# Layer 1's attention over all nodes: both row deviations multiplied into the value, gamma and beta applied to the sums

## The chip, the cores and the metric

The kernel runs on one core of a Trainium2 chip. The metric is the time of one execution in device microseconds. Before the change the median of 6 runs is 3528.72 us (3521.03 to 3540.67).

The engines are named as the profile names them: PE (TensorE matmul) and PEld (its weight load), DVE (VectorE), ACT (ScalarE), POOL (GpSimd) and SP (SyncE, which here only issues transfers). PSUM is the memory that matmuls write to.

## The reference, cut to what matters

A graph network of two layers works on 3125 nodes with 256 features and 100000 edges. Layer 1 adds to every node a sum over its neighbours (graph attention), an attention over all nodes that is linear in the queries, and then a mixture of experts. The change is in the second of these:

```python
q = _split_heads(seq @ wq.T, B, S)          # 4 heads of 64
k = _split_heads(seq @ wk.T, B, S)
v = _split_heads(seq @ wv.T, B, S)
k = _layer_norm(k, ln_k_g, ln_k_b)          # over the 64 of a head: (k - mu) * rsqrt(var + eps) * g + b
v = _layer_norm(v, ln_v_g, ln_v_b)
kv = jnp.einsum('bhsd,bhse->bhde', k, v) / S
ga = jnp.einsum('bhsd,bhde->bhse', q, kv)
return ga @ wo.T + bo
```

For each head `kv` is a 64 by 64 matrix, a sum over all nodes of the outer product of a normalized key and a normalized value.

## The kernel before, in words

**Tiles and blocks.** The 3125 nodes lie in 25 tiles of 128 rows (the last has 53). The edges are sorted by target and lie in 31 blocks (`NK`): block 0 and block 30 hold 7 gathers, every other block 28. The stage of interest is class `Layer1`; its order of instructions is written by hand, and each engine works through its own list in that order.

**A block** (`block`, L1562 to L1670) does the graph attention of its edges. At its top `run` (L1893) calls `gather` for the *next* block: 28 indirect transfers on POOL (L1555), each of 128 rows of 264 numbers, into the buffers `r0` (three of them) and `r1` (two). So gathers of the next block can start when the matmuls that read the old contents of those buffers are done (L1662, the `sums` of the block before). The block itself adds the two halves of the scores (L1581), finds maxima along runs of edges (L1590 to L1626, with PE transposes in L1594 and L1609), takes exponentials into `factors`, which lies in the PSUM tile `fixed` (L1631), multiplies the gathered rows by them (L1650: 128x4096, then 128x3072), builds one-hot matrices (L1653: `dl` compared with `self.row`, the numbers 0 to 31) and sums the messages with matmuls (L1662). `close`, `place` and `placed` add the result of the block before to the nodes (L1683, L1702, L1710).

**Units.** The other two parts of layer 1 are cut into units, generators that `yield` a nominal cost in us. `take(us)` (L1382) adds to a credit and lets units run until the credit is used up. A block calls it five times, with 2, 3, 3.5, 5 and 5 times `more` (L1616): `more` is 1.0 in block 0, 1.3 in blocks 1 to 6, and 1.0 from block 7 on (1.5 in the last ones). The queue of units begins with `keys` (the sums of `kv` over all tiles), then `mix` (folds `wo` and `wq` into them), then `mixing` (one matmul pair for each tile, which adds the attention to the nodes, L1872 and L1876), and then the experts, a group of tiles at a time, once these are complete. `run` calls `take(12)` before block 0.

**One tile of `keys`** (L1781 to L1809), as a pipeline of three steps:

- `products(t)`: the tile's transposed rows `xm` (loaded by SP, L1856, four buffers) times `wk` and `wv`, L1786, into a PSUM tile `yp` of 2x256 numbers (two buffers, shared with `place` and `mixing`). The means over a head are already taken out of the weights (L1776 to L1778).
- `normal_heads`: ACT squares (L1792), DVE sums the squares of each head (L1795), ACT takes the root (L1796), DVE the reciprocal (L1797), and then DVE multiplies by the reciprocal (L1800), by gamma (L1801) and adds beta (L1802), each over 128x512, into `h1` (two buffers). Gamma and beta of key and value lie on all partitions in an `xt` tile.
- `add(t)`: two matmuls for each tile, key against value, into `cps`, the right half of `fixed` (L1808).

PE's list has `products(t)`, then `add(t-2)`; DVE's has `normal_heads(t-1)` behind that. At the end (L1822) `cps` is scaled by 1/N and masked to the blocks of a head, and `mix` goes on from there.

`fixed` is one PSUM tile of 128x512 numbers: `self.row` in columns 0 to 31, `factors` in 32 to 255, `cps` in 256 to 511. A float32 matmul shows in the trace as two pairs of a weight load and a matmul.

Of the kernel before, what the change touches and what calls it, by code (L numbers as in the profile page):

```python
# [17 lines left out]
N, D, E = 3125, 256, 100000  # L18
P = 128
NB = 25  # L20
# [15 lines left out]
R, HD, DH = 8, 8, 32  # L36
# [7 lines left out]
def row_bc(v, n, start=0):  # L44

    return bass.AP(tensor=v.tensor, offset=v.offset + start, ap=[[0, P], [1, n]])
# [863 lines left out]
QD, QC, NQ = 32, 7, 118  # L910
# [3 lines left out]
NK = len(BQ)  # L914
# [25 lines left out]
GB = 3  # L940
# [330 lines left out]
class Layer1:  # L1271
# [290 lines left out]
    def block(self, b, part, A, N):  # L1562

        nc, C, wk, ps, B = self.nc, self.C, self.wk, self.ps, self.B
# [82 lines left out]
        for j, (s0, k, r, got) in enumerate(part):  # L1647
            n = nq * k
# [110 lines left out]
    def keys(self):  # L1759


        nc, wk, ps, C = self.nc, self.wk, self.ps, self.C
        ws = []
        xt = wk.tile([P, 2, GB * P], F32, name="xt")
        gb = xt[:, :, :P].rearrange("p j (i d) -> p j i d", i=2)
        heads = lambda x: x.rearrange("p i (h d) -> p i h d", d=64)
        for i, c in enumerate("kv"):
            w = load_k(nc, wk, self.a[f"L1_mix_w{c}T"], f"ew{i + 1}")
            for j, p in enumerate("gb"):
                nc.sync.dma_start(gb[:, j, i, :], row_bc(self.a[f"L1_mix_ln_{c}_{p}"], 64))  # L1770
            ws.append(w)
        for t in range(4):
            self.mixed_rows(t)
        for w in ws:
            mean = wk.tile([P, HD], F32, name="den").rearrange("p (i h) -> p i h", i=2)
            nc.vector.tensor_reduce(mean, heads(w), AX.X, OP.add)  # L1776
            nc.vector.tensor_scalar(mean, mean, -1.0 / 64, None, op0=OP.mult)
            nc.vector.tensor_tensor(heads(w), heads(w), mean[:, :, :, None].to_broadcast([P, 2, 4, 64]), OP.add)  # L1778
        yield 1.0

        def products(t):  # L1781
            x = self.xm.pop(t)
            kp = ps.tile([P, 2, D], F32, name="yp", bufs=2)
            for i in range(2):
                for k in range(2):
                    nc.tensor.matmul(kp[:, i, :], x[:, k, :], ws[i][:, k, :], start=(k == 0), stop=(k == 1))  # L1786
            self.mixed_rows(t + 4)
            return kp

        def normal_heads(kp):  # L1790
            sq = wk.tile([P, 2, GB * P], F32, name="h2")[:, :, :D]
            nc.scalar.activation(sq, kp, AF.Square)  # L1792
            var = wk.tile([P, HD], F32, name="den")
            v = var.rearrange("p (i h) -> p i h", i=2)
            nc.vector.tensor_reduce(v, heads(sq), AX.X, OP.add)  # L1795
            nc.scalar.activation(var, var, AF.Sqrt, bias=C.eps, scale=1.0 / 64)  # L1796
            nc.vector.reciprocal(var, var)  # L1797
            kv = wk.tile([P, 2, GB * P], F32, name="h1")[:, :, :D]
            sh = [P, 2, 4, 64]
            nc.vector.tensor_tensor(heads(kv), heads(kp), v[:, :, :, None].to_broadcast(sh), OP.mult)  # L1800
            nc.vector.tensor_tensor(heads(kv), heads(kv), gb[:, 0, :, None, :].to_broadcast(sh), OP.mult)  # L1801
            nc.vector.tensor_tensor(heads(kv), heads(kv), gb[:, 1, :, None, :].to_broadcast(sh), OP.add)  # L1802
            return kv

        def add(t, kv):
            n = P if t < NB - 1 else LAST
            for g in range(2):
                nc.tensor.matmul(self.cps[g], kv[:n, 0, g * P:(g + 1) * P], kv[:n, 1, g * P:(g + 1) * P],  # L1808
                                 start=(t == 0 and g == 0), stop=(t == NB - 1 and g == 1))  # L1809

        kp, kv = products(0), None
        yield 2.4
        for t in range(1, NB + 2):
            nxt = products(t) if t < NB else None
            if kv is not None:
                add(t - 2, kv)
# [951 lines left out]
```

## Time and profile before

| what | us |
|---|---|
| median of the 6 runs | 3528.72 |
| lowest, highest | 3521.03, 3540.67 |
| the profiled execution's own time | 3535.06 |
| its span, first to last instruction | 3533.3 |

The mean TensorE clock granted in the span is 0.825. Busy shares of the span: PE 67% (PEld 45%), DVE 50%, ACT 22%, POOL 29%. The chain of work that ended last, followed back from the end, is spread over many lines: PE 20%, "another core or an unknown queue" 13%, DVE 10%, issue 8%, ACT 3%, POOL 2%, DMA 2%.

Layer 1's blocks take the time from 1690 us to the end. In it `keys` runs from 1701 us to 1972 us, `mix` and `mixing` to about 2062 us.

How to read the views used below. In a *table of stretches* each row is a stretch of time with the busy us of each engine (and the number of instructions), the granted clock (1.00 is full), the share of the 16 DMA engines and the GB/s. In the *timeline* each row is start, duration, engine, line, operation, tiles, and in square brackets the idle time of that engine before it with what ended it: another instruction, "remote" (a semaphore that the profile cannot put down to anyone near it in time), or "issue" (nothing that the profile shows). A *view of one line* gives the number of its instructions, their duration in ns (minimum, median, maximum), first and last start, and the forms.

### The profile page before, as it was taken

The page shows a single profiled execution, that of the slowest core. Times are in us where ns is not written, and L with a number is a line of the kernel's source. Part 1 is how long each engine was busy: PE and PEld are TensorE (multiplying, and loading weights), DVE is VectorE, ACT ScalarE, POOL GpSimd, SP SyncE. Part 2 cuts the span into 40 slices and gives each one's busy share as a digit, 9 for nine tenths or more (in the row PEclk, how much of TensorE's full clock was granted, in tenths as well). Part 3 has the DMA queues.
Part 4 walks back from the last instruction along what each step waited for, and adds up shares of the span by engine and source line. Part 5 has one row for each costly group of instructions (what it writes and reads, how often), then busy time and mean ns, then how long its engine had stood idle before and what let it go on. Part 6 is the DMA issues. An engine that isn't in the chain of part 4 may idle for free.

```text
span 3533.3 us, 36506 instructions
## 1 busy us (share of the span) xinstructions
PE 2372.5 (67%) x12426; PEld 1579.8 (45%) x12426; DVE 1775.7 (50%) x4133; ACT 786.8 (22%) x1788; POOL 1026.4 (29%) x1075
## 2 busy tenths in 40 slices
PE   2788899999678999889245535535445554554576
PEld 1465544556466888544133324323223332333455
DVE  6999887566400212343266544456345446453552
ACT  2444022222211222222021112112112111121233
POOL 1000000011266000310533445365454455454400
PEclk9899999999788999899676767667668776687788
DMA  3333466332444667444522444344344344343434
GB/s 111 69 74 76 147 204 206 94 104 85 128 129 141 201 189 226 138 157 167 142 73 67 111 110 130 102 128 119 99 114 119 103 118 122 98 131 109 124 94 128
DMA packets 434699, 440.55 MB, mean 125 GB/s; under 512 B 167203, under 2 KB 380600, under 8 KB 434374
## 3 DMA queue, kind: packets, MB, share of 16 engines
q1 hardware_dynamic: 340160, 271.40, 25.7%
q0 software_dynamic: 50128, 130.98, 13.7%
q10 hardware_dynamic: 44214, 35.72, 3.8%
q8 instruction: 102, 1.67, 0.2%
q14 instruction: 95, 0.78, 0.1%
HBM read 337.49 MB, written 100.46 MB: 124 GB/s over the span
## 4 chain that ended last, share of the span: by engine, by line
PE 20%; another core or an unknown queue 13%; DVE 10%; issue 8%; ACT 3%; POOL 2%; DMA 2%; ACTq 0%; SPq 0%; DVEq 0%; POOLq 0%
PE hp L1420 7%; PE hp L2686 4%; PE yp L1480 3%; POOL r L1555 2%; PE sums L1662 2%; DVE r L1650 1%; DMA ew<-in_L_ffn_expert_w 1%; DVE own L1372 1%; ACT h L1423 1%; PE yp L1503 1%; PE hp L1412 1%; DVE ot L1351 0%; PE yp L1702 0%; DMA r<-tab,b_at 0%
## 5 line engine op out<-in xcount | busy, mean ns | idle before, releaser
L1555 POOL DMA_INDIRECT r<-tab,b_at x826 | 792.8, 960 | 1060.9 <-issue 397.4
L1420 PE MATMUL hp<-xt,ew 128*128 128x256 f32 (+2 forms) x576 | 195.7, 475 | 146.0 <-ACT h L1423 112.7
L2237 POOL DMA_INDIRECT route_x<-x,slot x50 | 50.6, 1012 | 812.8 <-DVE slot L2233 648.4
L1480 PE MATMUL yp<-ew,h 128*128 128x256 f32 x600 | 171.5, 434 | 156.3 <-issue 99.3
L2380 PE MATMUL fhp<-fxe,fw 128*128 128x256 f32 x960 | 240.3, 408 | 39.4 <-ACT fhid L2381 25.8
L1650 DVE TENSOR_TENSOR r<-r,fixed 128x4096 f32<-128x4096 f32 (+3 forms) x62 | 229.3, 3698 | 64.6 <-ACT fixed L1631 55.9
L1423 ACT ACTIVATE h<-hp,bc 128x256 f32<-128x256 f32 (+2 forms) x288 | 136.8, 481 | 556.9 <-PE hp L1420 243.6
L2380 PEld LDWEIGHTS fhp<-fxe,fw 128*128 128x128 f32 x960 | 188.1, 204 | 88.9 <-ACT fhid L2381 34.2
L2535 PE MATMUL agg<-at,py 128*128 128x512 bf16 (+4 forms) x1200 | 218.9, 336 | 1.6 <-issue 1.4
L2535 PE MATMUL agg<-at,px 128*128 128x512 bf16 (+2 forms) x1050 | 217.0, 358 | 1.9 <-DMA row_beta<-in_L_gnn_beta 1.9
L2388 PE MATMUL fyp<-fw,fhid 128*128 128x256 f32 x960 | 212.2, 379 | 0.0
L1480 PEld LDWEIGHTS yp<-ew,h 128*128 128x128 f32 x600 | 127.9, 221 | 186.9 <-issue 110.8
L1486 DVE SCALAR_TENSOR_TENSOR xs<-yp,wgt,xs 128x256 f32<-128x256 f32 x150 | 66.2, 478 | 282.8 <-PE yp L1480 171.8
L1420 PEld LDWEIGHTS hp<-xt,ew 128*128 128x128 f32 x576 | 115.6, 226 | 197.3 <-ACT h L1423 122.6
L2686 PE MATMUL hp<-wt,xt 128*128 128x512 f32 x400 | 186.6, 620 | 21.3 <-ACT xt L351 9.7
L1420 PE MATMUL hp<-h,ew 128*128 128x256 f32 (+2 forms) x576 | 178.6, 442 | 27.8 <-ACT h L1423 14.1
L2388 PEld LDWEIGHTS fyp<-fw,fhid 128*128 128x128 f32 x960 | 180.5, 190 | 22.9
L2381 ACT ACTIVATE fhid<-fhp,fb 128x256 f32<-128x256 f32 x240 | 112.6, 473 | 334.2 <-PE fhp L2380 206.8
L1662 PE MATMUL sums<-r,oh 128*32 128x264 f32 x1652 | 132.5, 439 | 39.9 <-DVE oh L1653 25.6
L2535 PEld LDWEIGHTS <-py 128*128 128x128 bf16 (+1 forms) x1200 | 111.6, 99 | 90.4 <-issue 7.2
L1420 PEld LDWEIGHTS hp<-h,ew 128*128 128x128 f32 x576 | 115.0, 220 | 74.1 <-issue 24.6
L2666 POOL DMA_INDIRECT y<-route_y,slot x50 | 49.3, 986 | 337.7 <-SPq L2637 307.2
(468 smaller groups left out, 3909.1 us busy)
## 6 DMA issues: line engine op xcount, KB each, us to landing
fw<-in_L_ffn_W SPq DMA_DIRECT2D x60, 1024.0 KB
ew<-in_L_ffn_expert_w SPq DMA_DIRECT2D x216, 256.0 KB
at<-adj SPq DMA_DIRECT2D x44, 640.0 KB
route_x<-zero SPq DMA_DIRECT2D x104, 256.0 KB
tab<-stage SPq DMA_DIRECT2D x25, 1056.0 KB
oe<-b_order ACTq DMA_DIRECT2D x117, 168.0 KB
adj<-adj_o SPq DMA_DIRECT2D x78, 250.0 KB
r<-tab,b_at POOLq DMA_INDIRECT x826
```

The lines of the kernel that those rows point to most:

```text
L1420: nc.tensor.matmul(hp[:, :W], ws[i, e][:, n, j * P:(j + 1) * P], x[:, n, :W], start=(n == 0), stop=(n == 1))
L1423: nc.scalar.activation(o[:, j, :W], hp[:, :W], AF.Relu, bias=b[:, e, j:j + 1])
L1480: nc.tensor.matmul(y[:, i - i0, :], h2[e][:, n, i * P:(i + 1) * P], ws[3, e][:, n, :], start=(n == 0), stop=(n == 1))
L1486: nc.vector.scalar_tensor_tensor(xs[:, t, :], y[:, i - i0, :], wgt[:, i, e:e + 1], xs[:, t, :], op0=OP.mult, op1=OP.add)
L1555: st = self.nc.gpsimd.indirect_dma_start(out=r[:, q, c, :], out_offset=None, in_=self.table, in_offset=bass.IndirectOffsetOnAxis(ap=self.B ...
L1650: nc.vector.tensor_tensor(rv, rv, factors[j][:, :, :, None].to_broadcast([P, n, HD, DH]), OP.mult)
L1662: mm = nc.tensor.matmul(self.sums[q * QD:(q + 1) * QD, :], oh[:, q, c, :], r[:, q, c, :], start=(s0 + c == 0), stop=(s0 + c == QC - 1))
L2380: nc.tensor.matmul(hp, w1[:, k, i * P:(i + 1) * P], xe[:, k, :], start=(k == 0), stop=(k == 1))
L2381: nc.scalar.activation(hid[:, i, :], hp, AF.Gelu, bias=b1[:, 0, i:i + 1])
L2388: nc.tensor.matmul(yp, hid[:, i, t * P:(t + 1) * P], w2[:, i, :], start=(i == 0), stop=(i == K1 - 1))
L2535: nc.tensor.matmul(agg[g][:, :cw], parts[j][:n, k, g * P:(g + 1) * P], at[:n, i, :cw], start=(k == 0 and j == 0), stop=(k == NB - 1 and j ...
L2686: nc.tensor.matmul(hp.rearrange("p r d -> p (r d)"), xt[:, k, :], wt[:, k, j * 512:(j + 1) * 512], start=(k == 0), stop=(k == 1))
```

## The change

1. `normal_heads` no longer normalizes the key. ACT copies the raw products of key and value to `h1`; DVE multiplies the two reciprocals of a row and head (128x4) and multiplies that into the raw value alone (128x256). Gamma and beta are left out.
2. `add` gains four matmuls for each tile: the raw key (and the raw value) of each half against the reciprocals, two columns each. They give the sums over all nodes of the normalized key and value without gamma and beta, `S`, which beta's cross terms need.
3. At the end gamma and beta are applied once to the sums: `kv` = gk gv C + gk bv (sum of k) + bk gv (sum of v) + N bk bv, with one more round over PE that spreads a row over the partitions.
4. `S` needs eight columns of the bank that `cps` accumulates in. It takes those of `self.row`; until `keys` is done, `self.row` is read from its copy in SBUF, and afterwards it is written to PSUM as before.
5. gamma and beta of the key are loaded as columns: six small transfers in place of four, behind the two weights.
6. `more` of blocks 1 to 6 goes from 1.3 to 1.15.

```diff
@@ __init__
-        self.row = fixed[:, :QD]
+        self.row = self.C.row[:, :QD]
+        self.kept_row = fixed[:, :QD]
...
-        nc.vector.tensor_copy(self.row, C.row[:, :QD])
@@ block
-        more = 1.3 if 0 < b < 7 else 1.0 if b < NK - 4 else 1.5
+        more = 1.15 if 0 < b < 7 else 1.0 if b < NK - 4 else 1.5
@@ keys
         def normal_heads(kp):
-            sq = wk.tile([P, 2, GB * P], F32, name="h2")[:, :, :D]
+            st = wk.tile([P, 2, GB * P], F32, name="h2")
+            sq, v, both = st[:, :, :D], st[:, :, D:D + 4], st[:, 0, D + 4:D + 8]
             nc.scalar.activation(sq, kp, AF.Square)
...
-            nc.scalar.activation(var, var, AF.Sqrt, bias=C.eps, scale=1.0 / 64)
-            nc.vector.reciprocal(var, var)
-            kv = wk.tile([P, 2, GB * P], F32, name="h1")[:, :, :D]
-            sh = [P, 2, 4, 64]
-            nc.vector.tensor_tensor(heads(kv), heads(kp), v[:, :, :, None].to_broadcast(sh), OP.mult)
-            nc.vector.tensor_tensor(heads(kv), heads(kv), gb[:, 0, :, None, :].to_broadcast(sh), OP.mult)
-            nc.vector.tensor_tensor(heads(kv), heads(kv), gb[:, 1, :, None, :].to_broadcast(sh), OP.add)
-            return kv
+            nc.scalar.activation(v, v, AF.Sqrt, bias=C.eps, scale=1.0 / 64)
+            kv = wk.tile([P, 2, GB * P], F32, name="h1")
+            nc.scalar.copy(kv[:, :, :D], kp)
+            nc.vector.reciprocal(v, v)
+            nc.vector.tensor_tensor(both, v[:, 0, :], v[:, 1, :], OP.mult)
+            nc.vector.tensor_tensor(kv[:, :, D:].rearrange("p g (h d) -> p g h d", d=64),
+                                    kp[:, 1, :].rearrange("p (g h d) -> p g h d", g=2, d=64),
+                                    both.rearrange("p (g h) -> p g h", g=2)[:, :, :, None]
+                                    .to_broadcast([P, 2, 2, 64]), OP.mult)
+            return kv, v
...
             for g in range(2):
-                nc.tensor.matmul(self.cps[g], kv[:n, 0, g * P:(g + 1) * P], kv[:n, 1, g * P:(g + 1) * P],
-                                 start=(t == 0 and g == 0), stop=(t == NB - 1 and g == 1))
+                c = slice(g * P, (g + 1) * P)
+                nc.tensor.matmul(self.cps[g], kv[:n, 0, c], kv[:n, g, D:], start=(t == 0 and g == 0),
+                                 stop=False)
+                for i in range(2):
+                    nc.tensor.matmul(S[:, i, g, :], kv[:n, i, c], v[:n, i, 2 * g:2 * g + 2], start=False,
+                                     stop=(end and g == 1 and i == 1))
...
         cx = self.mixed[0]
+        ones = wk.tile([P, 2, GB * P], F32, name="h2")
+        sel = wk.tile([P, 2, GB * P], F32, name="h1")
+        nc.vector.memset(ones[:, 0, :P], 1.0)
+        nc.vector.tensor_tensor(own, S, C.blocks[64][:, None, None, ::64].to_broadcast([P, 2, 2, 2]), OP.mult)
+        nc.vector.tensor_reduce(one_each[:, :, :, 0], own, AX.X, OP.add)
+        nc.vector.tensor_tensor(u[:, 0, :, 0], one_each[:, 0, :, 0], gk.to_broadcast([P, 2]), OP.mult)
+        bp = ps.tile([P, 2, P], F32, name="tp", tag="hp", bufs=2)
         for g in range(2):
-            nc.vector.scalar_tensor_tensor(cx[:, g, :], self.cps[g], 1.0 / N, C.blocks[64],
+            nc.vector.tensor_scalar(sel[:, g, :P], C.id, one_each[:, 1, g, :], None, op0=OP.mult)
+            nc.tensor.matmul(bp[:, g, :], ones[:, 0, :P], sel[:, g, :P], start=True, stop=True)
+        for g in range(2):
+            two = lambda x: x.rearrange("p (h d) -> p h d", d=64)
+            w, z = two(sel[:, g, P:2 * P]), two(ones[:, g, P:2 * P])
+            nc.vector.tensor_tensor(w, two(bp[:, g, :]), gv, OP.mult)
+            nc.vector.scalar_tensor_tensor(w, bv, float(N), w, op0=OP.mult, op1=OP.add)
+            nc.vector.scalar_tensor_tensor(z, two(self.cps[g]), gk, gv, op0=OP.mult, op1=OP.mult)
+            nc.vector.scalar_tensor_tensor(z, bv, u[:, 0, g, :], z, op0=OP.mult, op1=OP.add)
+            nc.vector.scalar_tensor_tensor(z, w, bk, z, op0=OP.mult, op1=OP.add)
+            nc.vector.scalar_tensor_tensor(cx[:, g, :], ones[:, g, P:2 * P], 1.0 / N, C.blocks[64],
                                            op0=OP.mult, op1=OP.mult)
+        nc.vector.tensor_copy(self.kept_row, C.row[:, :QD])
+        self.row = self.kept_row
         self.keyed = True
```

How many units fall into which block is fixed when the program is written, and follows from the credits (each row: what is in the block before and after the change):

| block | before | after |
|---|---|---|
| ahead of 0 | 4 products, 2 adds | the same |
| 0 | 6 products, 6 adds | the same |
| 1 | 7, 7 | the same |
| 2 | 8, 8 | 6, 6 |
| 3 | 2 adds, the end of `keys`, `mix`, 12 tiles of `mixing` | 2 products, 4 adds, the end, `mix`, 4 tiles |
| 4 | 13 tiles of `mixing` | 20 tiles |
| 5 | 12 expert matmuls (L1420) | 1 tile of `mixing`, 10 of them |
| 6 | 34 of L1420, 16 of L1480 | 32, 12 |
| 7 | 10, 8 | 14, 12 |

From block 8 on the units are the same.

More of the change, by code (lines that the diff above doesn't have):

```diff
@@ L1764, in keys @@
         xt = wk.tile([P, 2, GB * P], F32, name="xt")
-        gb = xt[:, :, :P].rearrange("p j (i d) -> p j i d", i=2)
+        gv, bv = (xt[:, j, None, :64].to_broadcast([P, 2, 64]) for j in range(2))
+        gk, bk = (xt[:, j, 64:65] for j in range(2))
+        own, one_each, u = (xt[:, 0, i:j].rearrange("p (i g c) -> p i g c", i=2, g=2)
+                            for i, j in ((72, 80), (80, 84), (84, 88)))
+        S = self.kept_row[:, :8].rearrange("p (i g c) -> p i g c", i=2, g=2)
         heads = lambda x: x.rearrange("p i (h d) -> p i h d", d=64)
@@ L1768, in keys @@
             w = load_k(nc, wk, self.a[f"L1_mix_w{c}T"], f"ew{i + 1}")
-            for j, p in enumerate("gb"):
-                nc.sync.dma_start(gb[:, j, i, :], row_bc(self.a[f"L1_mix_ln_{c}_{p}"], 64))
             ws.append(w)
+        for j, p in enumerate("gb"):
+            nc.sync.dma_start(xt[:, j, :64], row_bc(self.a[f"L1_mix_ln_v_{p}"], 64))
+            with nc.allow_non_contiguous_dma(reason="a column of 64"):
+                for h in range(2):
+                    nc.sync.dma_start(xt[h * 64:(h + 1) * 64, j, 64:65],
+                                      self.a[f"L1_mix_ln_k_{p}"].rearrange("(p o) -> p o", o=1))
         for t in range(4):
@@ L1790, in normal_heads @@
         def normal_heads(kp):
-            sq = wk.tile([P, 2, GB * P], F32, name="h2")[:, :, :D]
+            st = wk.tile([P, 2, GB * P], F32, name="h2")
+            sq, v, both = st[:, :, :D], st[:, :, D:D + 4], st[:, 0, D + 4:D + 8]
             nc.scalar.activation(sq, kp, AF.Square)
-            var = wk.tile([P, HD], F32, name="den")
-            v = var.rearrange("p (i h) -> p i h", i=2)
             nc.vector.tensor_reduce(v, heads(sq), AX.X, OP.add)
-            nc.scalar.activation(var, var, AF.Sqrt, bias=C.eps, scale=1.0 / 64)
@@ L1797, in normal_heads @@
-            nc.vector.reciprocal(var, var)
-            kv = wk.tile([P, 2, GB * P], F32, name="h1")[:, :, :D]
-            sh = [P, 2, 4, 64]
-            nc.vector.tensor_tensor(heads(kv), heads(kp), v[:, :, :, None].to_broadcast(sh), OP.mult)
-            nc.vector.tensor_tensor(heads(kv), heads(kv), gb[:, 0, :, None, :].to_broadcast(sh), OP.mult)
-            nc.vector.tensor_tensor(heads(kv), heads(kv), gb[:, 1, :, None, :].to_broadcast(sh), OP.add)
-            return kv
-        def add(t, kv):
+            nc.scalar.activation(v, v, AF.Sqrt, bias=C.eps, scale=1.0 / 64)
@@ L1806, in add @@
+            return kv, v
+        def add(t, kv, v):
             n = P if t < NB - 1 else LAST
+            end = t == NB - 1
             for g in range(2):
-                nc.tensor.matmul(self.cps[g], kv[:n, 0, g * P:(g + 1) * P], kv[:n, 1, g * P:(g + 1) * P],
-                                 start=(t == 0 and g == 0), stop=(t == NB - 1 and g == 1))
+                c = slice(g * P, (g + 1) * P)
[4 more added lines that the diff above has]
+                                     stop=(end and g == 1 and i == 1))
@@ L1815, in keys @@
             if kv is not None:
-                add(t - 2, kv)
+                add(t - 2, *kv)
             kv = normal_heads(kp) if t <= NB else None
```

## The prediction

> **What bounds the kernel now.** I read the granted clock first (one core, 0.825), then the chain that ended last: no engine holds more than 20% of it, but 13% is "another core or an unknown queue", so I looked for where waits end that nobody claims. That led to a table of stretches over layer 1's first blocks, cut where the gathers on POOL start and end.
>
> ```profile
> core 0: us, PE busy (x) PEld busy (x) DVE busy (x) ACT busy (x) POOL busy (x), PEclk, DMA share, GB/s
> 1802.00:1837.00 35.00, 10.52 (x51) 8.15 (x51) 15.53 (x37) 4.51 (x10) 26.77 (x28) 0.66 0.46 124
> 1837.00:1874.00 37.00, 24.10 (x123) 17.30 (x123) 28.69 (x43) 6.69 (x15) 0.11 (x1) 0.68 0.12 33
> 1874.00:1909.00 35.00, 12.18 (x53) 9.49 (x53) 11.44 (x27) 3.23 (x9) 26.78 (x28) 0.65 0.46 124
> 1909.00:1951.50 42.50, 25.32 (x135) 18.72 (x135) 34.14 (x51) 8.87 (x18) 0.17 (x1) 0.72 0.12 34
> 1951.50:1986.40 34.90, 7.79 (x46) 5.43 (x46) 19.57 (x37) 4.88 (x12) 26.61 (x28) 0.52 0.47 124
> 1986.40:2011.50 25.10, 20.16 (x122) 14.11 (x123) 10.91 (x18) 3.73 (x10) 0.03 (x1) 0.85 0.31 85
> ```
>
> A block is a **burst** of 28 gathers, always 35 us, and then a **window** without gathers. The next burst starts when PE has ended the block's sums. In bursts DVE is busy 11 to 20 of 35 us, so nothing that DVE saves there counts by itself. In the windows of blocks 1 and 2 (rows 2 and 4) DVE is busy 78% and 80%: these windows grow and shrink with the work. The timeline tells why bursts are slow; here block 1's:
>
> ```profile
> 1809.46 3.71 PE L1786 MATMUL yp<-ew,xm 128*128 128x256 f32 x8
> 1813.01 0.61 PE L1808 MATMUL fixed<-h 128*128 128x128 f32 x4
> 1823.26 0.60 ACT L1792 ACTIVATE h<-yp 128x512 f32<-128x512 f32 x1 [12.09 <-remote]
> 1829.68 0.69 DVE L1800 TENSOR_TENSOR h<-yp,den 128x512 f32<-128x512 f32 x1 [4.53 <-remote]
> 1841.69 0.60 ACT L1631 ACTIVATE fixed<-sc 128x128 f32<-128x128 f32 x2 [6.27 <-remote]
> ```
>
> PE's products end at 1813.2 by the page, the square that needs them starts at 1823.3; the next tile step waits until 1829.7, the exponentials until 1841.7, 4.7 us after the last gather. In a burst each release by PE comes some 6 to 16 us late, whatever DVE does. In the window the same step runs undisturbed:
>
> ```profile
> 1857.14 0.68 DVE L1795 TENSOR_REDUCE den<-h 128x8 f32<-128x512 f32 x1
> 1857.85 0.30 ACT L1796 ACTIVATE den<-den,eps 128x8 f32<-128x8 f32 x1 [2.56 <-DVE den L1795]
> 1858.19 0.20 DVE L1797 RECIPROCAL den<-den 128x8 f32<-128x8 f32 x1 [0.37 <-ACT den L1796]
> 1858.49 0.69 DVE L1800 TENSOR_TENSOR h<-yp,den 128x512 f32<-128x512 f32 x1
> 1859.22 0.69 DVE L1801 TENSOR_TENSOR h<-h,xt 128x512 f32<-128x512 f32 x1
> 1859.95 0.69 DVE L1802 TENSOR_TENSOR h<-h,xt 128x512 f32<-128x512 f32 x1
> ```
>
> From 1857.14 to 1860.56 a tile holds DVE 3.4 us, with one short hole for ACT's root. Before the change DVE bounds a tile in a window.
>
> **One tile.** Removed on DVE: three passes of 0.69, 2.08 us. Added on DVE: the value's product, 128x256 out of PSUM, 0.42 by L1683 (same size and source), and the product of the reciprocals, 128x4; the nearest row is L1680's 128x8, 0.15. Net -1.5 us of DVE for a tile, 38 us in all. Added on ACT: a copy of 128x512 out of PSUM, 0.60 as L1792. The copy and the value's product write the same `h1` tile, and in the changed program's list the product waits for ACT. So ACT's chain of a tile is square 0.60, (DVE's sum 0.68), root 0.30, copy 0.60, some 2.35 us with hand-overs of about 0.05; the product lies beside the next square.
>
> Added on PE: four matmuls of two columns, eight pairs. Two columns are not in the trace; the nearest rows are the router's six columns (L1434), with the same 128x128 weights, and L1808 with 128:
>
> ```profile
> L1434 PEld LDWEIGHTS lg<-rw,rh x50: 186/192/338, 2108.6 to 3495.3; 128*128 128x128 f32 x50
> L1434 PE MATMUL lg<-rw,rh x50: 171/254/360, 2109.0 to 3495.4; 128*128 128x6 f32 x50
> L1808 PE MATMUL fixed<-h x100: 272/378/582, 1718.1 to 1962.6; 128*128 128x128 f32 x96, 53*128 53x128 f32 x4
> ```
>
> These durations overlap; what counts is the distance. Four pairs of L1808 take 0.61 us with each 0.275 long, so one follows another after (0.61 - 0.275) / 3 = 0.11 us; at half clock they take 1.06 with 0.42, so 0.21. L1434's weight load has the lengths of L1808's, so I take 0.11 and 0.21 for a pair of two columns as well. By the same arithmetic L1786's eight pairs (1.97 and 3.76 us) stand 0.22 and 0.43 apart. PE's tile was 8 x 0.22 + 4 x 0.11 = 2.2 us at full clock and 4.3 at half; it becomes 3.05 and 6.0. [...]
>
> [...]
>
> So **PE takes DVE's place** as a tile's bound: 3.05 at full clock against 3.4. And the square of tile t now waits for the small matmuls of tile t-2 too, which read the reciprocals in the `h2` buffer that it writes; PE has them behind the products of t. That puts up to 4 x 0.11 + 8 x 0.11 = 1.3 us (2.5 at half clock) between products and square, where before the square went at once.
>
> **Blocks 0 and 1, windows** (11 tiles: six L1800 between 1768 and 1802, five between 1842 and 1872). I take 0.35 a tile: **-4 us**. Ends: all of DVE's 1.5 counts, -16; or PE runs at half clock half the time and each tile costs 0.9 more, +10. The 7.7 us of L1650 in a window, which DVE does between tiles, cover part of PE's extra work; I count that against the later square.
>
> **Block 2**, 8 tiles become 6. Ahead of L1622 there is one tile step fewer, so the scans need not wait for a square that comes at the end of the burst: tile and scans, from 1911.4 to 1918.0, go (-6.6); another tile of 3.4 falls out of the window; four remaining at 0.35. **-11 us**, between -5 (the waits take the tile's place) and -16.
>
> **Block 3** gets back two tiles (+6) with the scans behind them, and the new end: four small DVE steps of 0.15 to 0.2, two of 128x128 at 0.28 (L1688), PE's spread and its release (0.6 + 0.1), twelve of 128x128 at 0.28 (L1822), 5.5 us on the way to `mix`. Eight tiles of `mixing` leave it, four pairs of 0.22 each: -7. L1650, which ran inside the burst (1972.4), waits now for the last `add` behind it: +4.5, about the distance from the burst's end to the last release seen above. **+9 us**, between 0 and +16.
>
> **Block 4**: seven more tiles of `mixing`, 6 us of PE, half of them in the burst, which ends no later: **+3 us**, 0 to +6. Blocks 5 to 7 exchange two to four matmul groups; both sides of the exchange lie in blocks that cost 52 to 64 us: 0, within 3.
>
> **At nothing:** two more small loads on SP (0.45 each, 0.9 ahead of the first `xm`) and the weights before the gammas: first products start at 1709.7, in a burst that lasts to 1760, which hides either. `self.row` from SBUF: L1653 takes 0.68 for 128x512 out of PSUM, L1801 0.69 out of SBUF. `add` no longer waits for L1653's read of `fixed` but for L1650's, 0.6 earlier: at most 4 us over seven such places, behind the products that wait anyway. One more table load on ACT for the root, 1.3, in block 3's burst.
>
> Sum: -4 - 11 + 9 + 3 = **-3 us**. Against the profiled execution (3535.1) that is 3532; it lies 6.3 above the median of 3528.7, which becomes 3526. From block 8 on both programs issue the same, so a gain is carried to the end.
>
> **Rivals.** *DVE decides* (faster): PE stays warm and its work lies under L1650, so 1.5 a tile counts: blocks 0 and 1 -16, block 2 -15, block 3 +7, block 4 +3: -21, **3508**. For it: DVE at 80% in the windows. Against: PE is busy 24 to 25 us there too, and 5 tiles add 4.4. *PE at half clock decides* (slower): place, the two windows of blocks 1 and 2; price 0.9 a tile: +10, -7, +12, +3: +18, **3547**. It decides once the clock of these windows stays at or under the 0.68 and 0.72 granted now, since at half clock a tile costs PE 6.0. For it: eight pairs took 3.76 us at 1839, 1855 and 1867. Against: those followed idle time of PE, which the new matmuls fill.
>
> [...]
>
> *The bursts decide* (no change): all that windows gain is waited for in the next burst: 3529; it shares the forecast's interval.
>
> **Numbers.** Forecast with the last rival 0.50 (3515 to 3537), DVE decides 0.27, PE at half clock 0.20, the rest outside. Runs of this kernel cannot tell a change under about 0.3% (10.6 us) from none. Faster by more 0.28, within 0.50, slower 0.22. The range takes in the first rival's price and all but reaches the second's: 3505 to 3546.
>
> **What would show it.** Right: in the windows PE's busy share rises, DVE's falls, L1792's successor waits for PE; block 2 shorter by some 10 us, block 3 longer by as much; the copy's line 0.6, a two-column pair 0.11. Wrong: DVE still the fullest in the windows (first rival), the clock there under 0.7 with tiles over 4 us apart (second), or bursts that let fewer steps through than now, as each release there costs 6 us and nothing in the trace says what it depends on.

## The result and the profile after

The changed kernel takes **3550.02 us** (median of 20 runs, 3535.71 to 3562.22), the kernel before 3533.08 (median of 46, 3512.11 to 3547.12): ratio **1.0052, 95% interval 1.0040 to 1.0065**, some 18 us slower. The forecast was 3526, three us faster than before, and the range 3505 to 3546. The profiled execution spans 3556.8 us (before: 3533.3), at a mean granted clock of 0.820 (before: 0.825).

The table of stretches of the kernel after, cut where its bursts start and end: block 0's window, block 1's burst and window, block 2's burst and window, block 4's burst and window.

```profile
core 0: us, PE busy (x) PEld busy (x) DVE busy (x) ACT busy (x) POOL busy (x), PEclk, DMA share, GB/s
1760.50:1807.10 46.60, 28.78 (x167) 23.56 (x167) 24.62 (x68) 14.54 (x34) 0.14 (x1) 0.74 0.16 48
1807.10:1841.80 34.70, 14.66 (x81) 11.55 (x81) 10.85 (x28) 4.68 (x10) 26.47 (x28) 0.67 0.43 116
1841.80:1877.10 35.30, 24.41 (x149) 19.79 (x149) 21.64 (x38) 9.94 (x22) 0.03 (x1) 0.69 0.16 44
1877.10:1912.20 35.10, 18.30 (x86) 14.55 (x87) 10.95 (x29) 7.23 (x15) 26.85 (x28) 0.65 0.45 120
1912.20:1939.80 27.60, 21.13 (x126) 15.69 (x125) 19.52 (x33) 6.04 (x14) 0.00 (x0) 0.65 0.17 42
2012.60:2047.60 35.00, 11.95 (x58) 9.00 (x57) 10.37 (x25) 4.42 (x9) 26.73 (x28) 0.66 0.48 125
2047.60:2077.40 29.80, 21.88 (x120) 15.22 (x121) 19.37 (x27) 1.50 (x4) 0.00 (x0) 0.77 0.33 88
```

Against the rows of before: in block 1's window DVE falls from 78% to 61% and PE goes from 65% to 69%, as forecast, and the window is shorter (35.3 for 37.0). The loss lies elsewhere. Measured from the first gather (L1555) of one burst to that of the next, burst and window together are a block:

| block | before | after | e1 | e2 | e3 | e4 | e5 | e6 | e7 | e8 |
|---|---|---|---|---|---|---|---|---|---|---|
| 0 | 106.5 | 109.9 | 110.0 | 107.9 | 101.9 | 104.0 | 109.7 | 106.0 | 104.6 | 104.2 |
| 1 | 71.9 | 70.0 | 69.9 | 71.7 | 68.1 | 70.9 | 75.8 | 69.8 | 71.6 | 71.4 |
| 2 | 77.7 | 62.7 | 78.4 | 68.1 | 64.5 | 65.1 | 72.4 | 78.2 | 64.3 | 77.4 |
| 3 | 59.9 | 72.8 | 65.1 | 66.2 | 66.3 | 71.9 | 77.1 | 67.3 | 71.2 | 61.8 |
| 4 | 52.2 | 64.9 | 55.1 | 60.9 | 58.8 | 62.4 | 62.8 | 55.2 | 61.5 | 54.3 |
| 5 | 53.4 | 51.2 | 52.3 | 51.3 | 50.4 | 50.4 | 50.8 | 52.8 | 51.3 | 53.2 |
| 6 | 64.4 | 69.4 | 65.7 | 69.8 | 71.0 | 69.0 | 71.2 | 64.4 | 69.8 | 65.8 |
| 7 | 52.7 | 52.8 | 50.7 | 52.3 | 51.0 | 52.5 | 53.0 | 51.9 | 52.5 | 51.5 |
| sum | 538.8 | 553.7 | 547.1 | 548.2 | 532.2 | 546.3 | 572.7 | 545.6 | 546.8 | 539.5 |
| ratio of times | 1 | 1.0052 | 1.0030 | 1.0001 | 0.9977 | 1.0017 | 1.0065 | 1.0011 | 1.0010 | 0.9987 |

(e1 to e8 are experiments below; each column is one profiled execution. Kernels with the same units in blocks 0 and 1 repeat those blocks within 1.4: before and e2, after and e1. The sum is read as sharper than a whole run: all that follows block 7 has the same instructions and took 1281 to 1306 in the first six profiles. A difference of a few us between two sums is still not resolved.) Of the 15 us that the sum grows, block 4 has 12.7, block 3 12.9, block 6 5.0 and block 0 3.4; block 2 gives back 15.0 and blocks 1 and 5 4.1.

Block 0 first. A "release" below is the semaphore signal by which an engine lets another go on. The timeline of the kernel after, with the first three squares (ACT L1801), most of it inside the first burst (1697 to 1761):

```profile
1716.35 0.60 ACT L1801 ACTIVATE h<-yp 128x512 f32<-128x512 f32 x1 [23.77 <-DMA r<-tab,b_at]
...
1729.86 0.60 ACT L1801 ACTIVATE h<-yp 128x512 f32<-128x512 f32 x1 [11.39 <-issue]
...
1732.56 3.78 PE L1794 MATMUL yp<-ew,xm 128*128 128x256 f32 x8 [10.28 <-issue]
...
1743.99 0.29 PEld L1822 LDWEIGHTS fixed<-h,h 128*128 128x128 f32 x1 [2.51 <-issue]
1745.39 0.17 PE L1822 MATMUL fixed<-h,h 128*128 128x2 f32 x1 [2.43 <-issue]
1746.79 0.29 PEld L1822 LDWEIGHTS fixed<-h,h 128*128 128x128 f32 x1 [2.51 <-issue]
1748.19 0.16 PE L1822 MATMUL fixed<-h,h 128*128 128x2 f32 x1 [2.63 <-issue]
...
1769.39 0.60 ACT L1801 ACTIVATE h<-yp 128x512 f32<-128x512 f32 x1 [37.41 <-remote]
```

From 1744 to 1748 PE starts one instruction every 1.40 us, and the wait ahead of each is put down to "issue", to nothing that the profile shows: a two-column pair, 0.20 in the groups of four at 1814 and 1815 and 0.11 in those at 1833 and 1834 (0.85 and 0.51 for four, in the next burst), costs 2.8 here. The third square stands at 1769.4, behind the burst; in the kernel before (first burst 1695.5 to 1760.5) it ran inside:

```profile
1743.22 0.60 ACT L1792 ACTIVATE h<-yp 128x512 f32<-128x512 f32 x1 [20.21 <-issue]
```

So block 0's window does seven tiles and not six.

Block 4, the timeline of the kernel after, then that of before (L1650 starts the window's work, the 24 matmuls of L1662 end it):

```profile
2039.59 0.69 DVE L1710 TENSOR_TENSOR xs<-xs,yp 128x512 f32<-128x512 f32 x1 [16.23 <-remote]
...
2040.34 3.78 PE L1905 MATMUL yp<-m,xm 128*128 128x256 f32 x8 [15.30 <-DVE xs L1710]
...
2052.32 0.69 DVE L1909 TENSOR_TENSOR xs<-xs,yp 128x512 f32<-128x512 f32 x1 [9.37 <-remote]
2052.92 4.41 DVE L1650 TENSOR_TENSOR r<-r,fixed 128x4096 f32<-128x4096 f32 x1
...
2075.12 1.54 PE L1662 MATMUL sums<-r,oh 128*32 128x264 f32 x24
```

```profile
2042.09 0.69 DVE L1876 TENSOR_TENSOR xs<-xs,yp 128x512 f32<-128x512 f32 x1 [14.54 <-issue]
2042.69 4.41 DVE L1650 TENSOR_TENSOR r<-r,fixed 128x4096 f32<-128x4096 f32 x1
...
2061.35 1.54 PE L1662 MATMUL sums<-r,oh 128*32 128x264 f32 x24
```

Ahead of L1650 DVE sits idle 16 and 9 us before two steps that read what PE wrote to `yp` (L1702 for the first, to 2025.0; by the order of the two buffers the L1905 shown for the second, to 2044.1). PE had ended both 14.6 and 8.2 us before. In the kernel before one such idle time, of 14.5, stands there. Burst start to L1650 is 31.2 before and 40.3 after (+9.1), L1650 to the last sums 18.7 and 22.2 (+3.5): together the 12.7, within rounding.

### The profile page after: what moved, and what is told of

It reads as the page before. It is cut to its first block, busy times and chain, and to the rows that moved or that the text cites. A ratio compares the mean times of both kernels' runs of the same rounds, so it can differ in the third digit from the quotient of the medians.

```text
span 3556.8 us, 36947 instructions
## 1 busy us (share of the span) xinstructions
PE 2392.9 (67%) x12630; PEld 1607.7 (45%) x12630; DVE 1743.1 (49%) x4124; ACT 802.0 (23%) x1815; POOL 1025.0 (29%) x1075
## 4 chain that ended last, share of the span: by engine, by line
PE 21%; another core or an unknown queue 14%; issue 9%; DVE 8%; ACT 3%; DMA 2%; POOL 2%; ACTq 0%; DVEq 0%; SPq 0%; POOLq 0%
PE hp L1420 7%; PE hp L2719 4%; PE yp L1480 3%; PE sums L1662 2%; DVE r L1650 2%; POOL r L1555 1%; DMA ew<-in_L_ffn_expert_w 1%; PE yp L1503 1%; DMA r<-tab,b_at 1%; ACT h L1423 1%; DVE own L1372 1%; PE yp L1702 1%; PE hp L1412 1%; PE yp L1905 0%
## 5 line engine op out<-in xcount | busy, mean ns | idle before, releaser
L1555 POOL DMA_INDIRECT r<-tab,b_at x826 | 791.3, 958 | 1088.0 <-issue 418.4
L1420 PE MATMUL hp<-xt,ew 128*128 128x256 f32 (+2 forms) x576 | 190.3, 465 | 137.8 <-ACT h L1423 130.5
L1480 PE MATMUL yp<-ew,h 128*128 128x256 f32 x600 | 170.0, 431 | 167.3 <-issue 110.7
L1650 DVE TENSOR_TENSOR r<-r,fixed 128x4096 f32<-128x4096 f32 (+3 forms) x62 | 229.4, 3699 | 49.8 <-ACT fixed L1631 31.7
L1480 PEld LDWEIGHTS yp<-ew,h 128*128 128x128 f32 x600 | 125.7, 217 | 198.0 <-issue 121.6
L1420 PEld LDWEIGHTS hp<-xt,ew 128*128 128x128 f32 x576 | 114.7, 224 | 187.2 <-ACT h L1423 138.8
L1420 PE MATMUL hp<-h,ew 128*128 128x256 f32 (+2 forms) x576 | 178.9, 444 | 8.7 <-ACT h L1423 5.7
L1662 PE MATMUL sums<-r,oh 128*32 128x264 f32 x1652 | 131.0, 443 | 31.4 <-issue 22.4
L2568 PEld LDWEIGHTS <-px 128*128 128x128 bf16 (+1 forms) x1050 | 96.3, 98 | 104.9 <-issue 9.9
```

The source lines that it names most:

```text
L1420: nc.tensor.matmul(hp[:, :W], ws[i, e][:, n, j * P:(j + 1) * P], x[:, n, :W], start=(n == 0), stop=(n == 1))
L1480: nc.tensor.matmul(y[:, i - i0, :], h2[e][:, n, i * P:(i + 1) * P], ws[3, e][:, n, :], start=(n == 0), stop=(n == 1))
L1555: st = self.nc.gpsimd.indirect_dma_start(out=r[:, q, c, :], out_offset=None, in_=self.table, in_offset=bass.IndirectOffsetOnAxis(ap=self.B ...
L1650: nc.vector.tensor_tensor(rv, rv, factors[j][:, :, :, None].to_broadcast([P, n, HD, DH]), OP.mult)
L1662: mm = nc.tensor.matmul(self.sums[q * QD:(q + 1) * QD, :], oh[:, q, c, :], r[:, q, c, :], start=(s0 + c == 0), stop=(s0 + c == QC - 1))
L2568: nc.tensor.matmul(agg[g][:, :cw], parts[j][:n, k, g * P:(g + 1) * P], at[:n, i, :cw], start=(k == 0 and j == 0), stop=(k == NB - 1 and j ...
```

## The experiments

Two theories at the start: **credit** (the units stand in worse blocks) and **arithmetic** (PE's small matmuls and the later square cost). Times are given as ratios to runs of the kernel before beside them.

**e1, the credit undone.**

```diff
-        more = 1.15 if 0 < b < 7 else 1.0 if b < NK - 4 else 1.5
+        more = 1.3 if 0 < b < 7 else 1.0 if b < NK - 4 else 1.5
```

> The changed kernel with `more` of blocks 1 to 6 back at 1.3; the arithmetic stays new. Theory 'credit' (the loss of 17 us comes from which block each unit stands in: blocks 4 and 6 became 12.6 and 5.0 longer, and the new arithmetic costs about nothing): 3530 to 3537, no difference from the kernel before; block 4 (burst to burst) back at 52, block 2 between 70 and 78. Theory 'arithmetic' (the small matmuls at half clock and the later square cost 0.9 a tile over some 20 tiles, and the smaller credit wins back part of it in block 2): as slow as the changed kernel or slower, 3550 to 3565, with block 2 at 80 or more.

Measured: 3542.84, ratio 1.0030 (1.0009 to 1.0050). Block 4 is back at 55.1 and block 2 at 78.4, as the credit theory has it, and yet the kernel is slower than before: neither theory alone.

**e2, the credit alone** (the kernel before with 1.15).

> The kernel before with `more` of blocks 1 to 6 at 1.15 and nothing else. Theory 'credit': it carries the loss, 3545 to 3553; block 4 at about 64, block 2 at about 66, block 3 at about 70. Theory 'arithmetic': the credit alone is no loss, 3520 to 3534. If credit and arithmetic add up, this run and the one with the credit put back share out the 17 us between them.

Measured: 3541.49, ratio 1.0001 (0.9977 to 1.0024). The blocks move as the credit theory says (block 2 -9.6, block 3 +6.3, block 4 +8.7, block 6 +5.4; sum +9.5), the time as the other says; its interval just leaves room for 8. Over four pairs of kernels that differ in the credit alone the sum of blocks is 9.5, 6.6, 0.7 and 7.3 larger at 1.15 (before and e2, e1 and after, e6 and e4, e8 and e7). Their mean is 6, and I take the credit for some 6 us; no time by itself proves it.

**e3, without the small matmuls** (the kernel leaves out beta's cross terms).

```diff
-                for i in range(2):
-                    nc.tensor.matmul(S[:, i, g, :], kv[:n, i, c], v[:n, i, 2 * g:2 * g + 2], start=False,
-                                     stop=(end and g == 1 and i == 1))
...
+        nc.vector.memset(S, 0.0)
```

> The changed kernel without the four small matmuls of each tile (beta's cross terms are left out; the sums S are set to 0). It takes 8 pairs of PE from each of 25 tiles, 0.85 us for four at half clock by the trace, and the square's wait for them. Theory 'credit': the same as the changed kernel within 5, 3545 to 3552, since blocks 3 and 4 keep their units. Theory 'arithmetic': 1.7 us a tile in the windows, over about 20 tiles that stand there 20 to 30 less: 3520 to 3530.

Measured: 3526.45, ratio 0.9977 (0.9959 to 0.9995); sum of blocks 21.5 less than after, with the credit still at 1.15. The small matmuls, with what waits for them, are the loss and more than it.

**e4, the reciprocals in a tile of their own.**

```diff
-            sq, v, both = st[:, :, :D], st[:, :, D:D + 4], st[:, 0, D + 4:D + 8]
+            sq = st[:, :, :D]
+            dv = wk.tile([P, 12], F32, name="dv", bufs=4)
+            v, both = dv[:, :8].rearrange("p (i h) -> p i h", i=2), dv[:, 8:]
```

> The changed kernel with the reciprocals in a small tile of their own with four buffers, in place of columns of `h2`: the square of tile t no longer waits for the small matmuls of tile t-2. If that wait is the loss: 9 us of idle time of ACT is put down to it over four places, so 3535 to 3541. Theory 'credit', and theory 'arithmetic' by PE's time alone: within 4 of the changed kernel, 3546 to 3554.

Measured: 3538.00, ratio 1.0017 (0.9995 to 1.0039), as the wait theory has it. Its timeline, the third square and the copy behind it (the first burst starts at 1695.6):

```profile
1739.56 0.60 ACT L1803 ACTIVATE h<-yp 128x512 f32<-128x512 f32 x1 [16.95 <-remote]
...
1766.28 0.58 ACT L1807 COPY h<-yp 128x512 f32<-128x512 f32 x1 [25.07 <-remote]
```

The square is back inside the burst, six squares stand in the window, and block 0 is at 104.0; now the copy waits until behind the burst, as it writes what the small matmuls of two tiles before read.

**e5, e4 with every small matmul done twice** (the second time into `kept_row[:, 8:16]`).

> The reciprocals in a tile of their own (as in the run before) and every small matmul done twice, the second time into eight unused columns, so that the sums stay right. Read by the stretch from the first burst of layer 1 to the burst of its block 8, which leaves out the scatter of the rest: 602.7 us in the kernel before, 614.9 in the changed one, 593.1 without the small matmuls, 610.8 with the reciprocals in their own tile. Theory 'PE' (PE's own time for the small matmuls costs, 17.7 of that stretch): as much again, 624 to 632, and 3550 to 3560 in all. Theory 'wait' (only the square's wait for them costs, and PE's time lies beside other work): as with the own tile, 608 to 613, and 3534 to 3542.

Measured: 3592.89 where the kernel before takes 3566.48, ratio 1.0065 (1.0045 to 1.0086); the sum 26.4 above e4's. The stretch of the expectation, which takes in block 8 too, is 637.8, where the PE theory had 624 to 632. More small matmuls cost, and by more than that theory named; since e4's copy still waits for them, this does not part PE's own time from the releases behind it.

**e6, e4 with 1.3.**

> The reciprocals in a tile of their own and `more` back at 1.3. If the credit's price adds to that of the wait: the stretch from the first burst to block 8's at 602 to 606 (610.8 less the 6.4 that the credit alone gave back to the changed kernel), 3529 to 3534 in all, no difference from the kernel before. If the credit is worth nothing once the wait is gone: 609 to 612, and 3536 to 3541.

Measured: ratio 1.0011 (0.9993 to 1.0029), the stretch with block 8 610.7, as e4's: here the credit is worth nothing that these intervals could show.

**e7, half of the small matmuls folded in; e8, the same with 1.3.** `vv` lies in free columns of `xt`:

```diff
+                nc.tensor.matmul(both_sums[g], kv[:n, 0, c], vv[:n, g, :P + 2], start=(t == 0 and g == 0),
+                                 stop=False)
+                nc.tensor.matmul(SV[:, g, :], kv[:n, 1, c], vv[:n, g, P + 2:P + 4], start=False,
+                                 stop=(end and g == 1))
```

> The changed kernel with half of the small matmuls folded into the large ones: the key's two reciprocals of a half stand behind the 128 columns of the scaled value, so that one matmul of 130 columns gives that half's product and the key's sums; only the value's sums keep a matmul of two columns. Value and reciprocals lie outside `h2`, so the square waits for none of them. Four pairs of eight go. Theory 'PE': half of the 17.7 goes, the stretch at 600 to 604, 3526 to 3532 in all. Theory 'wait': 608 to 613, as with the own tile.

> The same with `more` at 1.3. If PE's time and the credit's price add up: the stretch at 594 to 598, 3520 to 3526 in all, faster than both kernels by 7 to 30 us. If only one of them is real: 601 to 606 and 3530 to 3536.

Measured: e7 1.0010 (0.9998 to 1.0022), stretch 611.7: a miss for the PE theory, four pairs fewer brought nothing against e4. e8 0.9987 (0.9970 to 1.0004), stretch 604.4, 6 less than e6: the fastest that computes all, but not shown to be faster than the kernel before. So there is no fixed price for a pair; that it goes by where the work falls is my reading, and no run shows it alone.

**e9, e10 and e12, the units behind L1650** (the edit made to the kernel after, to e8 and to the kernel before), and **e11, more PE instructions in blocks 10 to 22** (in the kernel after). Two further theories, on the late releases themselves: **backlog** (they fall behind with the number of PE's instructions in a burst) and **time** (they are late whatever stands ahead of them).

```diff
-        self.take(2 * more)
+        late = b < 7
+        self.take(0 if late else 2 * more)
         self.place()
-        self.take(3 * more)
+        self.take(0 if late else 3 * more)
...
-        self.take(3.5 * more)
+        self.take(0 if late else 3.5 * more)
...
-            self.take(5 * more)
+            self.take((9.25 if late else 5) * more)
```

```diff
         for i in range(2):
-            nc.tensor.transpose(lp[:nh, i, :], lf[:, i, :nh], C.id)
+            for _ in range(13 if 9 < b < 23 else 1):
+                nc.tensor.transpose(lp[:nh, i, :], lf[:, i, :nh], C.id)
```

> The changed kernel with the units of blocks 0 to 6 taken behind L1650 alone (credits 0, 0, 0, 9.25, 9.25 times `more` in place of 2, 3, 3.5, 5, 5): the same sum of credit, but no tile of `keys` or `mixing` between a burst's start and L1650. In the ten traces L1650 of a block starts 18 to 25 us ahead of its burst's end where 50 to 105 PE instructions (matmuls and weight loads) stand between the burst's start and it, and 4 to 32 us after the end in nearly every block where over 115 do; in the changed kernel blocks 0 to 4 have 299, 186, 190, 174 and 115. Theory 'backlog' (in a burst PE's releases fall behind with the number of PE's instructions): L1650 of blocks 1 to 6 at 15 to 22 us ahead of the end, the eight blocks from the first burst to block 8's 20 to 40 shorter than the changed kernel's 553.7, ratio 0.992 to 1.000. Theory 'time' (a release in a burst is late whatever stands ahead of it): L1650 stays behind the end, eight blocks within 8 of 553.7, ratio 1.003 to 1.008.

> The version with the folded matmuls and `more` 1.3 (ratio 0.9987, eight blocks 539.5), with the units taken behind L1650 as well. Theory 'backlog': 20 to 40 off, ratio 0.987 to 0.994, faster than both kernels. Theory 'time': 0.997 to 1.001.

> The kernel before with only the units moved behind L1650. Theory 'backlog': its blocks 0 to 2 have 231, 151 and 181 PE instructions ahead of L1650, block 3 has 90 and its L1650 runs inside the burst already, so it gains less than the changed kernel, 10 to 30: ratio 0.991 to 0.997. Theory 'time': 0.997 to 1.003. If it gains as much as the changed kernel does, the order of the units says nothing on why the change lost.

> The changed kernel with each of the two transposes of L1594 done 13 times in blocks 10 to 22 (24 more transposes, at least 48 PE instructions of some 0.1 us, 2.6 to 5 us of PE; the result is the same). There L1650 starts 18 to 25 us ahead of the burst's end, with 58 to 105 PE instructions ahead of it. Theory 'backlog': with 106 to 153 ahead of it, it starts between 8 us ahead of the end and 10 us after it, a shift of 12 to 30 us in most of the 13 blocks. Theory 'time': 3 to 6 us later, by PE's own time, still over 12 us ahead of the end.

Measured, and not expected: the kernel before took **2873.87 us** beside these. e9 2882.51, 1.0030 (1.0017 to 1.0043); e10 2872.96, 0.9999 (0.9978 to 1.0019); e12 2879.97, 1.0018 (1.0002 to 1.0033); e11 2860.33, once. In e9's timeline the third square starts 0.1 behind the end of the small matmuls it waits for (1650.63 and 1650.54). I take releases to have come promptly in all four, whose times lie together, so they do not speak on late ones. With prompt releases moving the units behind L1650 gained nothing (e12, the kernel before with that alone: 0.18% slower).

**x1 to x4: the changed kernel itself, e9, e10 and e11 again.**

> The changed kernel itself, so that the three others of this call have it beside them. On a chip where the kernel before takes some 3530 us: ratio 1.003 to 1.008, the eight blocks from the first burst 545 to 560. On a chip like the one of the last call, where it takes 2874 us and PE's releases come at once: theory 'arithmetic and credit cost by themselves': 1.003 to 1.006. Theory 'the loss is made by late releases': 0.998 to 1.002, since then the units moved and the small matmuls stand in bursts that hide them.

> The changed kernel with the units of blocks 0 to 6 behind L1650 (as before, on another chip). Where the kernel before takes some 3530 us, theory 'backlog': L1650 of blocks 1 to 4, now 45 to 50 us behind the block's first step, 10 to 15 us behind it as in the blocks from 10 on, 20 to 40 us less than the changed kernel. Theory 'time': the releases that moved behind L1650 are late there, and the eight blocks stay within 8 us of the changed kernel's.

> Folded matmuls, `more` 1.3 and the units behind L1650. Where the kernel before takes some 3530 us: theory 'backlog' 0.987 to 0.994; theory 'time' 0.997 to 1.001. On a chip with prompt releases: 0.998 to 1.002, as in the last call.

> The changed kernel with 24 more transposes of L1594 in each of blocks 10 to 22. On the chip with prompt releases L1650 came 2 to 3 us later by them, which is PE's own time. Where the kernel before takes some 3530 us, theory 'backlog': 10 to 30 us later in blocks 10 to 22; theory 'time': 3 to 6.

The kernel before took 2874.33 here. **x1 2872.22, ratio 0.9989 (0.9975 to 1.0003)**: without late releases the same program is not shown to be slower; the interval leaves room for 0.03%. x2 1.0016 (1.0002 to 1.0030), x3 0.9989 (0.9971 to 1.0007), x4 2871.23 once. x1's timeline shows the first tiles, the same instructions as above, also among gathers:

```profile
1644.06 0.60 ACT L1801 ACTIVATE h<-yp 128x512 f32<-128x512 f32 x1 [23.39 <-DMA r<-tab,b_at]
...
1646.08 0.60 ACT L1801 ACTIVATE h<-yp 128x512 f32<-128x512 f32 x1
...
1646.76 1.99 PE L1794 MATMUL yp<-ew,xm 128*128 128x256 f32 x8 [1.01 <-DVE h L1808]
...
1649.48 0.51 PE L1822 MATMUL fixed<-h,h 128*128 128x2 f32 x4
...
1650.08 0.60 ACT L1801 ACTIVATE h<-yp 128x512 f32<-128x512 f32 x1 [1.87 <-PE fixed L1822]
```

Square two follows square one by 2.0 us (13.5 above) and square three follows square two by 4.0 (39.5 above), 0.1 behind the end of the small matmuls (1649.99). In blocks 1 to 4 L1650 comes 23 to 27 us behind its block's first step (L1581), and 45 to 50 in the kernel after above. The chain on the page says the same; after, then x1:

```profile
PE 21%; another core or an unknown queue 14%; issue 9%; DVE 8%; ACT 3%; DMA 2%; POOL 2%; ACTq 0%; DVEq 0%; SPq 0%; POOLq 0%
```

```profile
PE 19%; DVE 10%; POOL 9%; issue 6%; DMA 5%; ACT 2%; SPq 0%; ACTq 0%; DVEq 0%; POOLq 0%
```

The waits that nobody claims are gone, POOL has 9% for 2%, and from 1943 us on 604 gathers run without a break. That is what the theory of the late releases had forecast (0.998 to 1.002). No trace of the kernel before itself with prompt releases is kept, so the blocks can't be set against each other there.

**y1 and y2: e9 and e11 once more.**

> The changed kernel with the units of blocks 0 to 6 behind L1650, for the third time; twice it fell on a chip with prompt releases, where it took 0.27% more than the changed kernel. Where the kernel before takes some 3530 us and releases come late: theory 'backlog': L1650 of blocks 1 to 4 at 10 to 20 us behind the block's first step, in place of 45 to 50, ratio 0.990 to 1.000. Theory 'time': 35 to 50 us behind it still, or the waits come back behind L1650, ratio 1.003 to 1.008.

> The changed kernel with 24 more transposes of L1594 in each of blocks 10 to 22; with prompt releases L1650 came 2 to 3 us later by them in most of the blocks. With late releases, theory 'backlog': 10 to 30 us later. Theory 'time': 3 to 6.

Prompt releases again (kernel before 2873.25): y1 1.0024 (1.0012 to 1.0035), y2 2866.04 once. What they show of prompt releases: L1650 comes 11 us behind its block's first step in blocks 1 to 3 and not 24, and yet the kernel's ratio is above x1's; and 48 more PE instructions leave L1650 of blocks 10 to 22 where it was on the mean (18.2 to 18.5 us behind that step, 18.5 in x1), so that the 2 to 3 us that the expectations of x4 and y2 name are not borne out. Whether the number of PE instructions makes releases late where they are late stays open: no run of these two edits met that.

## Why the prediction was wrong

**The step that failed.** Work put into a burst was taken as hidden, although the prediction had seen that releases there come 6 to 16 us late. It stands in the sum twice: in blocks 0 and 1, where only tiles in windows were priced (-4, measured +1.5), and in block 4, where half of seven tiles of `mixing` lay "in the burst, which ends no later" (+3, measured +12.7). The runs showed in its place that such work lengthens the waits for releases in the burst, so that steps fall behind its end: in block 0 a square 26 us later and one tile more in the window, in block 4 L1650 9.1 us later. What was right and what was off, term by term:

**The bound and its sign.** The rates were right. Four pairs of two columns take 0.51 with 0.17 each at full clock (granted 1.00 from 1863.4 to 1877.1), 0.85 with 0.25 at half (0.50 from 1841.8 to 1863.4): 0.11 and 0.20 a pair (taken: 0.11 and 0.21). The copy takes 0.565 (0.60), the value's product 0.425 (0.42), the product of the reciprocals 0.16 (0.15). In block 0's window a tile follows a tile in 4.76 for 5.02 before (squares from 1777.4 to 1801.2, and 1771.1 to 1796.2): -0.26, and -0.35 was forecast.

**Blocks 0 and 1: +1.5 in place of -4.** What failed is the count of tiles: 11 in windows, taken as given whatever PE does in the bursts. The square's new wait was priced at 1.3 to 2.5 us; in the first burst it moved a square by 26 (by 24.5 from the burst's start), and one tile more fell into block 0's window: 4.8 less 5 x 0.26 comes to 3.5, and 3.4 was seen. e4 takes the wait away and gets block 0 to 104.0.

**Block 2: -15.0 for -11.** Right: e1, with eight tiles in it, has 78.4.

**Block 3: +12.9 for +9**, inside the ends. The new end takes 6.0 (1991.3 to 1997.3; 5.5 forecast), and L1650 starts 9.2 behind the burst, not 4.5.

**Block 4: +12.7 for +3**, outside its ends (0 to +6) and the term most off. "Half of them in the burst, which ends no later" was true of the burst and beside the point: the burst ends on time (35.0), the releases in it do not (14.6 and 8.2 late), and L1650 waits for them (+9.1). e2 has 8.7 of it with the credit alone.

**Blocks 5 to 7: +2.9 for 0 within 3.**

In sum +15 for -3 in these blocks; the 8.5 more by which the two profiled spans differ lies ahead of them or in instructions that are the same. The rival "PE at half clock" had 3547, near the time, by a wrong sum: it laid +10 on blocks 0 and 1 (+1.5 measured) and +3 on block 4. Its 0.9 a tile does not follow from its own numbers either: halfway between 3.05 and 6.0, less 3.4, is 1.1. Its sign of being wrong did come: the clock in the windows of blocks 1 and 2 is 0.69 and 0.65 (0.68 and 0.72 before), with most tiles over 4 us apart, though PE is busier there; its stricter condition, at or under the values of before, held in block 2 alone. Each of these two clocks is a mean of two stretches: 0.50 up to 1863.4 and up to 1931.7, while PE's groups still have gaps of up to 1.2 and 1.6 us between them, and 1.00 from there to the window's end, 4.0 and 7.9 us into work without a gap over 0.2. So the new matmuls did not fill PE's gaps as the prediction had counted on. The last warning, bursts that let fewer steps through, is what came; it had been given no price.

**What is shown and what is not.** Shown: without the small matmuls there is no loss, and with twice as many there is more (e3, e5); and the same program is slower than the kernel before by 0.4 to 0.65% where releases are late and not by more than 0.03% where they are prompt (x1). Nearly shown: a good part of the loss is the square's wait (e4, whose interval, 0.9995 to 1.0039, just clears the 1.0040 of the changed kernel). Only argued: the credit's 6 us, on single traces; and that the late releases, and nothing else that differs between these two conditions, make the difference. The traces also differ in the clock (0.820 and 0.895), for which no run shows the cause, and in what bounds the rest: from 1943 us on the gathers of x1 follow each other without a break. Open: what makes releases late, what is behind one PE instruction every 1.40 us, and why folding half of the matmuls (e7) brought nothing.

## What to carry to other kernels

Work that was added to PE in stretches where its releases came late (14.6 and 8.2 us in block 4) was not hidden by them, though PE was idle there for the most part (busy 12.0 of 35.0 us in block 4's burst) and the stretches ended on time (block 4's burst 35.0, 35.1 before). Price such work by how late its own releases get and who stands behind them, and look for the waits that nobody claims. An operand put into a buffer that a later step writes tied that step to the operand's last reader (ACT's square waited 9.1 us for the small matmuls in four places, by the trace of the kernel after); a small tile of its own took half (by the blocks) to two thirds (by the times) of this loss away. Where a measurement's condition can change by a fifth, as here (2874 us for 3533), read ratios taken side by side only, and say under which condition a gain or loss was seen.

## What the runs showed of the hardware that was not expected

- In a burst with late releases PE's own instructions can come slowly as well: one every 0.70 or 1.40 us from 1739 to 1754, and so again from 1911.8 to 1916.7 at the end of block 2's burst and 4.5 us past it. In the groups of four between, from 1813.9 to 1900.4 inside and outside of bursts, the same pairs stand 0.11 to 0.20 apart, in x1 among gathers 0.11.
- The kernel before ran in two conditions that the program does not choose: 3511 to 3582 us, with most blocks from the eighth on at 48 to 59, and 2862 to 2887 us. In the second the changed kernel does 604 gathers in a row in 783 us, so 36 for the 28 of a block. The DMA engines moved the same bytes (440.5 MB) in both and a gather took as long on POOL (0.96 us). The number of the chip on record does not tell the two apart: e1 to e4 and y1 and y2 have the same one, the first four with late releases, the other two with prompt ones.
